# Layer 0 of a graph kernel: program order on VectorE, and twelve buffers of adj

## The chip, the cores and the metric

One core of one Trainium2 chip runs the whole program. The metric is device time in microseconds. Engines are named as in the profile: PE is TensorE's matmul row, PEld its weight loads, DVE VectorE, ACT ScalarE, POOL GpSimd, SP the engine that only issues transfers. DMA issues stand in the queues of SP, ACT and POOL beside their other work.

## The reference

Two graph layers over N = 4096 nodes with F = 512 features, one dense matrix `adj` with some 0.8% of its entries set (and the diagonal):

```python
# layer 0
h = relu(layernorm(x))
d = where(adj.sum(1) > 0, adj.sum(1) ** -0.5, 0)
x = x + relu((d[:, None] * adj * d[None, :]) @ h @ W0 + b0)
# layer 1
h = relu(layernorm(x))
g = h @ W1                                   # only g @ a[:F] and g @ a[F:] are used
e = leaky_relu((g @ a[:F]) + (g @ a[F:]).T, 0.2)
p = softmax(where(adj > 0, e, -1e12), axis=1)
q = -softmax(where(adj > 0, -e, -1e12), axis=1)
x = x + elu(concat([p @ h, q @ h], 1) @ wtrans)
```

## The kernel before

**Layer 0 is dense.** The 4096 output rows are 32 blocks of 128. The first phase (group 0, blocks 28 to 31) runs 32 rows of 128 nodes: for each it normalizes x on ACT and DVE, turns it on PE, multiplies it by W0 (`project`), and adds its product with the transposed adj into four PSUM banks (`multiply`). Beside that it streams the whole of `adj` in chunks of 128 x 1024 (`load_adj`, four a row, issued by SP into the pool `ain`): ACT sums a chunk (`junk`, line 747) for the degrees, DVE writes a 0/1 mark (line 748), and PE counts marks (`tally_up`) into a tally that says which nodes a half block of layer 1 needs. A chunk's buffer is free when its sum and its mark are done. The pool has 9 buffers.

Groups 1 to 8 (`GROUPS`: 4, 2, 4, 4, 4, 4, 4 and 2 blocks) compute the other 28 blocks by a Strassen scheme: for each of 16 steps jp, `load_at` brings the transposed adj (SP), `sum_at` makes four sums of its quarters on DVE (pool `sums`, three buffers; a two-block group makes them every second step), and `multiply_blocks` runs seven products for each pair of blocks on PE. A four-block group holds seven of the eight PSUM banks. When a group ends, the next one's first steps finish it: `join_blocks` puts its products together on DVE and `affine` scales them (group 0 needs `affine` alone, through `evict`), and at steps 0 to 3 `finish0` makes one block's x1 and its normalized row h: DVE and ACT take turns, ACT writes h (line 711, two buffers), two dots of h follow on DVE (line 895), h is written to one table by POOL's queue and to seven others by ACT's (line 465), and last DVE copies the second dot into t_all (line 905). A buffer of h is free when its eight writes have landed. The rows of the last two groups go to one table only. At step 12 `spread_s` turns s_all on PE (line 910) and sends it to memory.

Within a step the program traces the sums of step jp+1, at jp = 0 the joins, then the products of step jp, then `finish0`, then `step(jp)`.

**Lists.** `step` also takes items from two lists of work. `listing` holds, for each of two sides, eight beginnings (`block_codes` twice, `join_codes`, `count_nodes` four times, `make_places`), 73 rounds of `list_round`, and an end (`rows_and_joins`) for each of seven classes. A round finds the next eight entries of a class in each partition (lines 410 and 412) in a window of the 512 columns given by `place`. `joining` holds the transfers that POOL issues to put the lists into memory (`join`, line 432, each waiting for the one before) and `deal`, which brings them back and turns them into indices for layer 1.

**Layer 1 is sparse.** For each half block POOL gathers the listed rows of a table (line 473), DVE and ACT make the weights, and PE multiplies (line 516 and line 1397). The gathers of the first pair stand in group 8. A verdict, computed on the chip, says whether the lists were complete; if not, a dense layer 1 runs instead.

**Order.** The order of each engine's instructions is fixed when the program is compiled: a scheduler plays the program through with estimated times and takes what is ready, earlier traced work first. `keep_in_program_order(i)` ties i behind the one instruction that was traced just before it on its engine; it adds no wait of its own. Without it an instruction is placed where the scheduler finds its inputs ready.

**Weights.** `load_weights` loads a and W1 (transposed) by ACT's queue, at row 24 of the first phase; `weight_rows` multiplies them at row 30 (line 692) and spreads the result over all partitions as wa_bc (`wa`), which the dots of `finish0` read.

Of the kernel before, what the change touches and what calls it, by code (L numbers as in the profile page):

```python
# [19 lines left out]
P = 128  # L20
# [247 lines left out]
def gcn_gat_kernel(  # L268
# [118 lines left out]
    def place(c, n, side):  # L387


        p = SHARES[c]  # L390
        return (n + side * 8 * (n * (1 - p)) ** 0.5) / p

    def window(n):
        c, r = steps[n]
# [3 lines left out]
    def list_round(g, n):  # L398


        c, r = steps[n]
        if r == 0:
            keys[g] = make_pool.tile([P, EN], F32, tag="key", name=f"key{g}_{c}")
            lst[g] = make_pool.tile([P, max(CAPS)], F32, tag="lst", name=f"lst{g}_{c}")
            nc.vector.scalar_tensor_tensor(
                keys[g], codes[g], float(CODES[c]), rank, ALU.is_equal, ALU.mult
            )
        lo, hi = window(n)
        key, top = keys[g][:, lo:hi], lst[g][:, 8 * r : 8 * r + 8]
        nc.vector.max(top, key)  # L410
        if r + 1 < CAPS[c] // 8:
            nc.vector.match_replace(key, top, key, 0.0)

    def count_listed(g, c, lst):
        one = make_pool.tile([P, EN], F32, tag="flag16", name=f"listed{g}_{c}")[:, : CAPS[c]]
# [4 lines left out]

    def table_rows(g, c, lst):

        li = make_pool.tile([P, max(CAPS)], F32, tag="li", name=f"li{g}_{c}", bufs=2)
        li = li[:, : CAPS[c]]
        nc.vector.tensor_scalar(li, lst[:, : CAPS[c]], -1.0, base, ALU.mult, ALU.add)
        return li
# [11 lines left out]

    def deal(g):

        rows = make_pool.tile([P, EN], F32, tag="flag16", name=f"deal{g}")[:, : NH * STR // P]
        i = nc.gpsimd.dma_start(
            out=rows.rearrange("r (c p) -> r c p", p=P),
            in_=lst_dram[g].rearrange("(c r p) o -> r c (p o)", r=P, p=P),
        )
        turned = bank(f"deal_ps{g}")
        for c in range(NH * STR // P // P):
            part = slice(c * P, (c + 1) * P)
            nc.tensor.transpose(turned[:, part], rows[:, part], ident)
        nc.vector.tensor_copy(idx[g].rearrange("p b k -> p (b k)"), turned[:, : NH * STR // P])  # L450
        return i
# [108 lines left out]
    with sbuf(name="y0", bufs=1) as y_pool, sbuf(name="wa", bufs=1) as wa_pool, sbuf(name="bits", bufs=4) as bits_pool, sbuf(name="small0", bufs=4) as small, ExitStack() as rest, ExitStack() as lists:  # L560
# [109 lines left out]
            one(off[g], o, start, None, ALU.add)  # L670

        def load_bias(ln_pool):
            b_row = ln_pool.tile([1, F], F32, tag="b_row", name="b_row", bufs=1)
            nc.scalar.dma_start(out=b_row, in_=b0)
            nc.gpsimd.partition_broadcast(b_bc, b_row)

        def load_weights(ln_pool):

            a_sb = small.tile([P, 2 * FC], F32, tag="a_sb", name="a_sb", bufs=1)
            tc.keep_in_program_order(nc.scalar.dma_start(out=a_sb, in_=a_cols))  # L680
            w1t = []
            for c in range(FC):
                w1t.append(ln_pool.tile([P, F], F32, tag="w1t", name=f"w1t{c}", bufs=FC))
                tc.keep_in_program_order(
                    nc.scalar.dma_start(out=w1t[c], in_=w1_t[c * P : (c + 1) * P, :])
                )
            return a_sb, w1t

        def weight_rows(ln_pool, a_sb, w1t):
            wp = bank("wa_ps")  # L690
            for c in range(FC):
                nc.tensor.matmul(
                    wp[0:2, :], a_sb[:, c::FC], w1t[c], start=c == 0, stop=c == FC - 1
                )
            row = ln_pool.tile([2, F], F32, tag="wa_row", name="wa_row", bufs=1)
# [135 lines left out]

        def affine(y, acc, j):

            nc.vector.scalar_tensor_tensor(y, acc, d_all[:, j : j + 1], b_bc, ALU.mult, ALU.add)  # L834
            return y

        def new_y(work, j):
# [8 lines left out]
        def join_blocks(i0, n, acc, work, new_w):  # L846

            ys = {}
            for x in range(n // 2):
                p16, p23, p45, p7 = acc[x]  # L850
                j0, j1 = i0 + x, i0 + n // 2 + x
                ys[j0], ys[j1] = y, v = [new_y(work, j) for j in (j0, j1)]
                w = new_w(f"w{j0}")[:, :H]
                nc.vector.tensor_copy(y[:, :H], p16[:, :H])
                nc.vector.tensor_tensor(w, p16[:, H:], y[:, :H], ALU.add)  # L855
                nc.vector.tensor_tensor(y[:, H:], p45[:, H:], w, ALU.add)

                def first(p23=p23, y=y):
                    nc.vector.tensor_tensor(y, p23, y, ALU.add)  # L859

                def second(p7=p7, w=w, p45=p45, v=v):
                    two = "p (a f) -> p a f"
                    nc.vector.tensor_tensor(w, p7, w, ALU.add)
                    nc.vector.tensor_tensor(
                        v.rearrange(two, a=2),
                        p45.rearrange(two, a=2),
                        w.unsqueeze(1).to_broadcast([P, 2, H]),
                        ALU.add,
                    )
# [12 lines left out]
            return ys  # L882
# [70 lines left out]
        def sum_at(pool, at, n, name):  # L953

            a = blocks_of(at, n)
            q, w = a.shape[1], a.shape[4]
            t = pool.tile([P, 4, q, w], F32, tag="sums", name=name)
            op = nc.vector.tensor_tensor
            op(t[:, 0], a[:, :, 0, 1], a[:, :, 1, 1], ALU.add)
            op(t[:, 1], t[:, 0], a[:, :, 0, 0], ALU.subtract)  # L960
            op(t[:, 2], a[:, :, 0, 0], a[:, :, 0, 1], ALU.subtract)
            op(t[:, 3], a[:, :, 1, 0], t[:, 1], ALU.subtract)  # L962
            return t
# [34 lines left out]
                    seventh(x)  # L998

        i0, n = GROUPS[0]  # L1000
        with sbuf(name="w0", bufs=1) as w0_pool, sbuf(name="ain", bufs=9) as ain, sbuf(name="xs", bufs=5) as x_pool, sbuf(name="at6", bufs=5) as at_pool, sbuf(name="bits6", bufs=3) as bits6, sbuf(name="ln", bufs=3) as ln_pool, sbuf(name="marks", bufs=6) as mark_pool:
            dummy = ain.tile([P, RC], F32, tag="ain", name="dummy")
            dummy = dummy[:, : NH * STR // P]
            nc.gpsimd.memset(dummy, float(EN))
# [43 lines left out]
            for j in range(NJ):  # L1048
                tally_up(j)
                if j + 4 < NJ:  # L1050
                    load_x(x_pool, nc.gpsimd, j + 4)
                if j + 1 < NJ:
                    load_adj(ain, j + 1)
                    ats[j + 1] = load_at(at_pool, i0, n, j + 1, 1)
                    if j:
                        yps[j + 1] = project(w0_sb, j + 1)
                    sum_adj(j + 1, j < 3)
                if j == 3:
                    load_bias(ln_pool)
                if j == NJ - 8:  # L1060
                    vectors = load_weights(ln_pool)
                if j == NJ - 2:
                    weight_rows(ln_pool, *vectors)
                turn = partial(turn_x, ln_pool, j + 3, j < 2) if j < NJ - 3 else None
                multiply(acc, j, ats[j], turn)
                if j + 1 < NJ:
                    scale(yps.pop(j + 1), j + 1)
                pack(bits6, i0, j, ats.pop(j), j < 2)
        pending = (GROUPS[0], partial(evict, i0, acc))
        listing, joining = [], []  # L1070
        verdict = None
# [101 lines left out]
        with sbuf(name="work0", bufs=2) as work, sbuf(name="sums", bufs=3) as sum_pool, sbuf(name="at", bufs=6) as at_pool:  # L1173
# [29 lines left out]
        with sbuf(name="work2", bufs=2) as work, sbuf(name="sums2", bufs=2) as sum_pool, sbuf(name="at2", bufs=4) as at_pool, sbuf(name="scratch", bufs=1) as scratch, sbuf(name="pair", bufs=1) as pair:  # L1203
# [21 lines left out]
            def s_of0(r):  # L1225
                return s_pair[:, r % 2 * RB : (r % 2 + 1) * RB]

            def weights0(r):
# [274 lines left out]
```

## Time and profile before

| | us |
|---|---|
| median of 14 runs | 2152.63 (2143.09 to 2159.93) |
| the profiled execution | 2156.47 |
| its span | 2154.7 |
| first phase, to the first product of group 1 | 0 to 315.9 |
| groups 1 to 8 | 315.9 to 1056.9 |
| first half blocks of layer 1, from there | 1056.9 to 1170 |
| the rest of layer 1 | 1170 to 2154.7 |

PE is busy 1956.8 us (91%), DVE 1281.8 (59%), POOL 937.6 (44%), ACT 633.1 (29%). The page's digits by slices of 54 us:

```profile
PE   7998999889999999799865989989899999989988
PEld 3433348778788888688521333333333333333333
DVE  6554568979854388934443645655564546555561
...
PEclk9999999999999999999986999999999999999999
DMA  9887868386384747383758788888778888777760
```

Each digit is a tenth of busy share. Slices 0 to 5 are the first phase, slices 6 to 19 the groups, the rest layer 1. DVE is fullest in slices 6 to 10 and 15 to 16.

The rounds of the lists, and where they ran:

```profile
L410 DVE MAX8 lst<-key x146: 326/632/695, 371.4 to 897.3; 128x8 f32<-128x440 f32 x20, 128x8 f32<-128x480 f32 x14, 128x8 f32<-128x496 f32 x12, 128x8 f32<-128x488 f32 x12
...
busy tenths in 40 slices 0000000212100012200000000000000000000000
```

The three times are shortest, median and longest in ns. They fill slices 7 to 10 and 14 to 16 and are absent between: the scheduler has not spread them as the program lists them.

### The profile page before, as it was taken

How to read it: one execution, taken by the hardware profiler on the slowest of the kernel's cores; microseconds unless marked ns; L12 is line 12 of the kernel's file. 1: busy time of each engine (PE TensorE's matmuls, PEld its weight loads, DVE VectorE, ACT ScalarE, POOL GpSimd, SP SyncE). 2: the span in 40 equal slices, each digit the busy share in tenths (PEclk: the TensorE clock that was granted, in tenths of full speed). 3: DMA queues.
4: the chain of work that ended last, by engine and by line, in shares of the span. 5: the costliest groups of instructions: out<-in, count | busy, mean ns of one | idle time of the engine just before them, and what ended most of it. 6: DMA issues, size and time to landing. Idle time of an engine off the chain costs nothing.

```text
span 2154.7 us, 23721 instructions
## 1 busy us (share of the span) xinstructions
PE 1956.8 (91%) x7832; PEld 1079.9 (50%) x7832; DVE 1281.8 (59%) x2907; ACT 633.1 (29%) x1181; POOL 937.6 (44%) x1047
## 2 busy tenths in 40 slices
PE   7998999889999999799865989989899999989988
PEld 3433348778788888688521333333333333333333
DVE  6554568979854388934443645655564546555561
ACT  5765642112122212120221322322222223322221
POOL 3001001233321132331556667667666667766740
PEclk9999999999999999999986999999999999999999
DMA  9887868386384747383758788888778888777760
GB/s 364 308 302 263 301 207 311 92 265 216 100 312 139 269 160 254 98 282 97 228 172 290 244 279 254 268 272 254 259 249 268 252 276 254 238 248 247 238 196 21
DMA packets 181115, 503.53 MB, mean 234 GB/s; under 512 B 27091, under 2 KB 35699, under 8 KB 180982
## 3 DMA queue, kind: packets, MB, share of 16 engines
q0 software_dynamic: 73184, 275.36, 40.2%
q1 hardware_dynamic: 77808, 171.80, 23.6%
q10 hardware_dynamic: 29990, 54.75, 7.2%
q8 instruction: 64, 1.05, 0.2%
q14 instruction: 69, 0.57, 0.1%
HBM read 409.89 MB, written 103.02 MB: 238 GB/s over the span
## 4 chain that ended last, share of the span: by engine, by line
PE 43%; issue 5%; POOL 2%; DVE 1%; DMA 1%; ACT 0%; another core or an unknown queue 0%; DVEq 0%; POOLq 0%
PE u L516 31%; PE o L1397 10%; POOL g L473 2%; PE tp L550 2%; DMA g<-table,idx 0%; PE cs L540 0%; DMA table<-h 0%; DVE prod L895 0%; DVE stb L455 0%; DVE y L834 0%; DVE y L887 0%; DVE p L509 0%; POOL table L821 0%; ACT L499 0%; DVE y L859 0%
## 5 line engine op out<-in xcount | busy, mean ns | idle before, releaser
L473 POOL DMA_INDIRECT g<-table,idx x704 | 706.4, 1003 | 326.6 <-issue 207.6
L516 PE MATMUL u<-g,p 128*64 128x512 f32 x2816 | 701.7, 622 | 94.2 <-issue 77.6
L516 PEld LDWEIGHTS u<-g,p 128*64 128x64 f32 x2816 | 214.9, 142 | 525.1 <-issue 503.1
L972 PE MATMUL p<-t,sums 128*128 128x256 f32 x896 | 268.4, 384 | 12.3 <-DVE sums L960 7.8
L972 PE MATMUL p<-y,at 128*128 128x256 f32 x896 | 272.3, 386 | 2.3 <-DVE w L855 1.2
L972 PE MATMUL p<-y,sums 128*128 128x256 f32 x896 | 270.6, 384 | 0.4 <-DVE sums L962 0.4
L1397 PE MATMUL o<-wt_sb,ut 128*128 128x512 f32 x512 | 225.4, 593 | 0.5 <-ACT ut L555 0.5
L432 POOL DMA_INDIRECT ld<-li,off x112 | 101.7, 908 | 255.1 <-DMA ld<-li,off 196.6
L812 ACT ACTIVATE m<-at 128x1024 uint8<-128x1024 f32 x110 | 115.0, 1053 | 331.3 <-DMA at<-in_adj_t 273.9
L1367 DVE TENSOR_REDUCE total<-p 128x128 f32<-128x1792 f32 x62 | 201.9, 3257 | 2.1
L972 PEld LDWEIGHTS p<-t,sums 128*128 128x128 f32 x896 | 171.6, 193 | 40.3 <-DVE sums L960 11.1
L972 PEld LDWEIGHTS p<-y,at 128*128 128x128 f32 x896 | 171.3, 193 | 30.1 <-issue 2.7
L972 PEld LDWEIGHTS p<-y,sums 128*128 128x128 f32 x896 | 172.8, 193 | 25.1 <-DVE sums L962 0.8
L509 DVE SCALAR_TENSOR_TENSOR p<-g,p 128x384 f32<-128x384 uint8 (+1 forms) x256 | 145.5, 618 | 26.3 <-issue 13.8
L747 ACT ACTIVATE junk<-ar 128x1024 bf16<-128x1024 f32 x128 | 134.7, 1052 | 73.9 <-DMA ar<-in_adj 72.6
L821 POOL DMA_DIRECT2D table<-m x71 | 56.5, 796 | 225.4 <-ACT m L812 138.7
L1397 PEld LDWEIGHTS o<-wt_sb,ut 128*128 128x128 f32 x512 | 94.8, 190 | 108.5 <-issue 107.0
L1383 ACT ACTIVATE us<-u,rl 128x512 f32<-128x512 f32 x62 | 42.6, 688 | 360.0 <-PE u L516 145.7
L1405 DVE TENSOR_SCALAR eo<-o 128x512 f32<-128x512 f32 x32 | 22.1, 691 | 211.3 <-remote 80.0
L972 PE MATMUL p<-t,at 128*128 128x256 f32 x448 | 135.7, 385 | 9.8 <-DVE w L855 8.7
L487 DVE TENSOR_TENSOR z<-g,s 128x512 f32<-128x512 f32 (+1 forms) x124 | 77.8, 628 | 112.2 <-DMA g<-table,idx 97.3
L499 ACT ACTIVATE p<-z 128x512 f32<-128x512 f32 (+2 forms) x252 | 123.4, 548 | 70.4 <-issue 38.4
(198 smaller groups left out, 1937.5 us busy)
## 6 DMA issues: line engine op xcount, KB each, us to landing
ar<-in_adj SPq DMA_DIRECT2D x128, 512.0 KB
at<-in_adj_t SPq DMA_DIRECT2D x112, 512.0 KB
table<-h ACTq DMA_DIRECT2D x182, 258.0 KB
table<-m POOLq DMA_DIRECT2D x55, 256.0 KB
g<-table,idx POOLq DMA_INDIRECT x704
at<-in_adj_t SPq DMA_DIRECT2D x32, 256.0 KB
xr<-in_x SPq DMA_DIRECT2D x32, 256.0 KB
x1d<-y POOLq DMA_DIRECT2D x32, 256.0 KB
```

The source lines that it names most:

```text
L432: return nc.gpsimd.indirect_dma_start(out=lst_dram[g][:, :], out_offset=bass.IndirectOffsetOnAxis(ap=off[g][:, e, c : c + 1], axis=0), in_ ...
L473: i = nc.gpsimd.indirect_dma_start(out=gt[:, k, :], out_offset=None, in_=table[2 * n // RPT], in_offset=bass.IndirectOffsetOnAxis(ap=idx[n ...
L487: return nc.vector.tensor_tensor(z, t.to_broadcast([P, n, RB]), s.unsqueeze(1).to_broadcast([P, n, RB]), ALU.add)
L499: i = nc.scalar.activation(p[:, :, :, g], z, AF.Exp, scale=(1.0, -1.0)[g])
L509: nc.vector.scalar_tensor_tensor(e, m, 0.0, e, ALU.is_gt, ALU.mult)
L516: i = nc.tensor.matmul(u[h * RB : (h + 1) * RB], p[:, k, h].rearrange("p g i -> p (g i)"), row(k), start=k == HALVES[r % 2][h][0], stop=en ...
L747: nc.scalar.activation(junk, ar, AF.Identity, accum_out=part[:, c : c + 1]),
L812: nc.scalar.activation(m, at, AF.Sign)
L821: nc.gpsimd.dma_start(out=rows_of(t, e)[:, c:, ROW_W + (a - t * TT) * P // 4 : ROW_W + (b - t * TT) * P // 4], in_=masks[i0][:, c:, (a - i ...
L972: i = nc.tensor.matmul(out, left[:, x * P : (x + 1) * P], right, start=jp == 0 and first, stop=jp == NP - 1 and (final or not first),)
L1367: nc.vector.tensor_reduce(total, q, AX.X, ALU.add)
L1397: nc.tensor.matmul(po, ut[:, g, c, :], wt_sb[:, g * FC + c, :], start=g == 0 and c == 0, stop=g == 1 and c == FC - 1,)
```

## The change

1. `list_round`'s two instructions, `affine`, every instruction of `join_blocks` and the four of `sum_at` are tied to program order, and so are the scores of the second half block in `weights0` at the end of layer 0.
2. The pool `ain` has 12 buffers. To make room, the four W1 tiles take `ain` buffers and two short rows share one buffer. `load_weights` moves from row 24 to row 30, `weight_rows` behind the loop.
3. The lower edge of a round's window is 6 instead of 8 deviations from the mean; the upper stays at 8.
4. One list item a step is taken in group 2 too, where none was, and two joins a step always, where it was one or two. `li` has three buffers, and `deal` has a tile of its own.

```diff
-        return (n + side * 8 * (n * (1 - p)) ** 0.5) / p
+        return (n + side * (7 + side) * (n * (1 - p)) ** 0.5) / p
...
-        nc.vector.max(top, key)
+        tc.keep_in_program_order(nc.vector.max(top, key))
         if r + 1 < CAPS[c] // 8:
-            nc.vector.match_replace(key, top, key, 0.0)
+            tc.keep_in_program_order(nc.vector.match_replace(key, top, key, 0.0))
...
-        li = make_pool.tile([P, max(CAPS)], F32, tag="li", name=f"li{g}_{c}", bufs=2)
+        li = make_pool.tile([P, max(CAPS)], F32, tag="li", name=f"li{g}_{c}", bufs=3)
...
-        rows = make_pool.tile([P, EN], F32, tag="flag16", name=f"deal{g}")[:, : NH * STR // P]
+        rows = make_pool.tile([P, NH * STR // P], F32, tag="deal", name=f"deal{g}")
...
-        def load_weights(ln_pool):
+        def load_weights(ain):
...
-                w1t.append(ln_pool.tile([P, F], F32, tag="w1t", name=f"w1t{c}", bufs=FC))
+                w1t.append(ain.tile([P, RC], F32, tag="ain", name=f"w1t{c}")[:, :F])
...
-            nc.vector.scalar_tensor_tensor(y, acc, d_all[:, j : j + 1], b_bc, ALU.mult, ALU.add)
+            tc.keep_in_program_order(
+                nc.vector.scalar_tensor_tensor(y, acc, d_all[:, j : j + 1], b_bc, ALU.mult, ALU.add)
+            )
...
+            def op(*args):
+                tc.keep_in_program_order(nc.vector.tensor_tensor(*args))
+
...
-                nc.vector.tensor_copy(y[:, :H], p16[:, :H])
-                nc.vector.tensor_tensor(w, p16[:, H:], y[:, :H], ALU.add)
-                nc.vector.tensor_tensor(y[:, H:], p45[:, H:], w, ALU.add)
+                tc.keep_in_program_order(nc.vector.tensor_copy(y[:, :H], p16[:, :H]))
+                op(w, p16[:, H:], y[:, :H], ALU.add)
+                op(y[:, H:], p45[:, H:], w, ALU.add)
...
             t = pool.tile([P, 4, q, w], F32, tag="sums", name=name)
-            op = nc.vector.tensor_tensor
+            def op(*args):
+                tc.keep_in_program_order(nc.vector.tensor_tensor(*args))
+
...
-        with sbuf(name="w0", bufs=1) as w0_pool, sbuf(name="ain", bufs=9) as ain, sbuf(name="xs", bufs=5) as x_pool, sbuf(name="at6", bufs=5) as at_pool, sbuf(name="bits6", bufs=3) as bits6, sbuf(name="ln", bufs=3) as ln_pool, sbuf(name="marks", bufs=6) as mark_pool:
+        with sbuf(name="w0", bufs=1) as w0_pool, sbuf(name="ain", bufs=12) as ain, sbuf(name="xs", bufs=5) as x_pool, sbuf(name="at6", bufs=5) as at_pool, sbuf(name="bits6", bufs=3) as bits6, sbuf(name="ln", bufs=3) as ln_pool, sbuf(name="marks", bufs=6) as mark_pool:
...
-                if j == NJ - 8:
-                    vectors = load_weights(ln_pool)
                 if j == NJ - 2:
-                    weight_rows(ln_pool, *vectors)
+                    vectors = load_weights(ain)
...
                 pack(bits6, i0, j, ats.pop(j), j < 2)
+            weight_rows(ln_pool, *vectors)
...
-                    n = 0 if b == 2 or not 0 < jp < 14 else 1 if b == 1 else 2 + jp % 2
-                    for todo, n in ((listing, n), (joining, 1 + jp % 2)):
+                    n = 0 if not 0 < jp < 14 else 1 if b < 3 else 2 + jp % 2
+                    for todo, n in ((listing, n), (joining, 2)):
...
-                    scores(s_of0(r), z[:, k : k + n], gt[:, :, ROW_T : ROW_T + 1].bitcast(F32))
+                    i = scores(s_of0(r), z[:, k : k + n], gt[:, :, ROW_T : ROW_T + 1].bitcast(F32))
+                    if r == blocks[1]:
+                        tc.keep_in_program_order(i)
```

More of the change, by code (lines that the diff above doesn't have):

```diff
@@ L672, in load_bias @@
         def load_bias(ln_pool):
-            b_row = ln_pool.tile([1, F], F32, tag="b_row", name="b_row", bufs=1)
+            b_row = ln_pool.tile([1, F], F32, tag="row", name="b_row", bufs=1)
             nc.scalar.dma_start(out=b_row, in_=b0)
             nc.gpsimd.partition_broadcast(b_bc, b_row)
-        def load_weights(ln_pool):
+        def load_weights(ain):
             a_sb = small.tile([P, 2 * FC], F32, tag="a_sb", name="a_sb", bufs=1)
@@ L694, in weight_rows @@
                 )
-            row = ln_pool.tile([2, F], F32, tag="wa_row", name="wa_row", bufs=1)
+            row = ln_pool.tile([2, F], F32, tag="row", name="wa_row", bufs=1)
             nc.scalar.copy(row, wp[0:2, :])
@@ L853, in join_blocks @@
                 w = new_w(f"w{j0}")[:, :H]
-                nc.vector.tensor_copy(y[:, :H], p16[:, :H])
-                nc.vector.tensor_tensor(w, p16[:, H:], y[:, :H], ALU.add)
-                nc.vector.tensor_tensor(y[:, H:], p45[:, H:], w, ALU.add)
+                tc.keep_in_program_order(nc.vector.tensor_copy(y[:, :H], p16[:, :H]))
+                op(w, p16[:, H:], y[:, :H], ALU.add)
+                op(y[:, H:], p45[:, H:], w, ALU.add)
                 def first(p23=p23, y=y):
-                    nc.vector.tensor_tensor(y, p23, y, ALU.add)
+                    op(y, p23, y, ALU.add)
                 def second(p7=p7, w=w, p45=p45, v=v):
                     two = "p (a f) -> p a f"
-                    nc.vector.tensor_tensor(w, p7, w, ALU.add)
-                    nc.vector.tensor_tensor(
+                    op(w, p7, w, ALU.add)
+                    op(
                         v.rearrange(two, a=2),
```

## The prediction

> **What bounds the kernel now.** I read the page first (PE busy 91%, its last digits full), then the waits of TensorE, then a table by stage, cut where the traced blocks of layer 0 begin. Its columns are stretch, length, busy time with instruction counts of PE, weight loads, DVE, ACT, POOL, then granted clock, DMA share and GB/s.
>
> ```profile
> 43.90:93.10 49.20, 48.97 (x172) 21.05 (x172) 28.71 (x96) 35.77 (x77) 5.16 (x7) 1.00 0.91 336
> 93.10:312.00 218.90, 202.75 (x649) 83.09 (x652) 117.12 (x335) 132.30 (x262) 15.72 (x23) 0.99 0.79 267
> ...
> 315.90:424.60 108.70, 100.96 (x469) 87.17 (x468) 100.31 (x298) 24.81 (x29) 20.76 (x31) 0.95 0.64 215
> 424.60:483.70 59.10, 51.75 (x227) 44.41 (x226) 47.96 (x142) 10.84 (x17) 20.49 (x28) 0.91 0.78 256
> 483.70:585.70 102.00, 98.56 (x452) 84.70 (x451) 93.99 (x245) 19.78 (x22) 39.41 (x49) 1.00 0.49 160
> 585.70:687.50 101.80, 99.38 (x451) 85.89 (x450) 49.20 (x139) 20.69 (x25) 15.76 (x26) 0.98 0.63 215
> 687.50:785.80 98.30, 98.30 (x473) 85.87 (x472) 59.70 (x188) 20.68 (x25) 22.84 (x34) 1.00 0.64 215
> 785.80:891.30 105.50, 100.09 (x451) 85.67 (x450) 92.68 (x259) 20.47 (x25) 31.76 (x45) 0.98 0.59 200
> 891.30:1002.40 111.10, 101.06 (x455) 86.51 (x453) 47.59 (x140) 16.12 (x21) 29.27 (x41) 0.97 0.51 172
> ```
>
> The first two rows are the first phase, the others groups 1 to 7. Group 5, at 98.3 us, is a four-block group in which PE never waits; a two-block group would take half, 49.2. Against this, groups 1 to 7 lose 10.4, 9.9, 3.7, 3.5, 0, 7.2 and 12.8 us, together 47.5. They lose where DVE is nearly always busy (100.3 of 108.7 us in group 1) or stood full of list rounds just before. The longest waits of PE are:
>
> ```profile
> PE p L972 <- DVE w L855: 9.9, 4, 6.7
> PE s_ps L910 <- DVE prod L895: 7.4, 1, 7.4
> PE s_ps L910 <- DVE o L669: 7.3, 1, 7.3
> ```
>
> So VectorE's order costs layer 0 up to 47 us. From 1170 us the digits show PE full; the later layer moves as a block, by when group 8 ends.
>
> In the first phase a row of 128 adj rows has 28 matmul records (counts, yp and acc 8 each, tx 4). The fast stretch does 172/28 = 6.1 rows at 8.0 us; the long one, less the 8 records of wa_ps, 641/28 = 22.9 rows at 9.56, with a DMA share of 0.79. The queue of SP tells why:
>
> ```profile
> SPq L735 <- DVE mark L748: 169.9, 72, 7.7
> ...
> 208.86 2.13 SPq L735 DMA_DIRECT2D ar<-in_adj  x4
> ```
>
> The columns of a wait are total, times, longest; those of the timeline start and length. Four loads leave together here, and the next at 218.95, 10.1 us on, when a batch of marks frees their buffers; ACT then waits for them (3.11 us at 213.80), its row sum waits, d_all waits, and the next marks stand behind d_all on DVE. It is a loop through the buffers.
>
> **Twelve buffers.** Chunk 4x+3 of adj now waits for the mark of 12 chunks earlier, not 9, so for one batch of marks earlier: the loop opens. Bounds per row: nothing, if DMA is the limit, to 9.56 - 8.0 = 1.56 us, the rate of the fast stretch (34 us over 22 to 23 rows). From 100 to 125 us the share is 0.88 at 293 GB/s, only a tenth above the long stretch's 267; I take 0.83 us a row, between the ends: 23 x 0.83 = **-19 us**.
>
> **The weights, moved.** load_weights goes from row 24 to row 30: five ACT issues, past the ACT work of six rows; 0, for the weights are wanted only after the last row. weight_rows goes behind the loop: its eight matmul records (304.62 to 308.2, 3.6 us of PE) run once as before, its ACT copy (0.58) and three ACT issues go past one row: 0. But wa_bc lands later: now the copy is at 308.25 and its two broadcasts are issued at 311.38. Moved behind the last matmul (316), the first dot of group 1, some 11 us in, just covers it; without that cover it costs 0 to 4. SP's loads for group 1 today wait 15.6 us for wa_ps, whose weights lie where those loads land. If the first load still does, PE waits for landing (308.24 to 312.25) and two sums, 4.8 us. Between 0 and 8.8 in all: **+2**.
>
> **Lists.** A round is (88.0 + 78.0 + 11.7)/146 = 1.22 us of DVE, by the busy times of lines 410 and 412. The narrower lower edge takes the columns that one side's rounds scan, by the formula, from 59,592 to 53,616; at 1.06 ns a column (0.35 us for 184 columns at 818.10, 0.68 for 496 at 850.73) that is 12.7 us of DVE for both sides, 1.13 us a round; it is hidden behind PE except where a round stands in a sum below. Each side has 73 rounds, 7 ends and 8 beginnings, 176 items in all. They go at 1 a step in groups 1 and 2, then 2 or 3, and end in group 7. The lists' third li buffer removes a DVE wait of 4.08 us (at 879.49, inside group 6's loss). Deal's own tile: nothing of DVE waits for it by the trace; 0.
>
> **The pins.** The losses above should shrink, since rounds no longer crowd. But a pinned instruction follows the DVE instruction traced just before it. The sums of step k stand behind finish0 of step k-2 (its last DVE instruction copies t_all) and that step's list rounds. The copy waits for a dot, the dot for ACT's h, and h for the buffer that eight table writes must leave. Group 5 shows the times:
>
> ```profile
> 697.24 0.15 DVE L905 COPY t_all<-h 128x1 f32<-128x1 f32 x1
> ...
> 708.24 0.15 DVE L905 COPY t_all<-h 128x1 f32<-128x1 f32 x1
> ...
> 713.45 0.14 DVE L905 COPY t_all<-h 128x1 f32<-128x1 f32 x1
> ...
> 722.39 0.81 ACT L711 ACTIVATE h<-y,rrb 128x512 f32<-128x512 f32 x1 [10.94 <-DMA table<-h]
> ...
> 724.64 0.15 DVE L905 COPY t_all<-h 128x1 f32<-128x1 f32 x1
> ```
>
> That is 9.7, 20.7, 26.0 and 37.1 us after the group's first product. A step lasts 98.3/16 = 6.1 us; PE wants two sums (0.8 us) of step 5 at 30.9. Behind the fourth copy and three rounds (3.4) they come at 37.1 + 3.4 + 0.8 = 41.3: 10.4 us late, where today those sums ran at 714.5, 27 us in. Bounds for the fourth copy: if ACT issues the second tile's seven writes right after the first's (6.1 us each set, landing 7.3 us after, by 703.2 and the wait that ends at 710.5), it falls to about 32.8, 6.1 us late; at 42.5 (groups 4 and 6) 15.8. I take 35, between group 5's row and the better order: 8.3 late.
>
> Each such wait also lowers the clock: the 1.96 us wait at 588.65 is followed by a granted 0.86 over 586 to 598, so 3.4 us at half, 1.7 lost. Two waits a group: 3.4. A head then costs 11.7.
>
> The Trainium skill, in "TensorE: Matmul & The Clock Gate" under "HAM oscillation — how this bites in real kernels", has it that only idle gaps above about 3.4 us bring the slow clock back. The 1.96 us row differs from it (a 2.05 us wait at 946.68, with a clock of 1.00 after it, agrees). By the rule waits of 2 to 3 us cost no clock, and the total below would be an estimated 14 us less.
>
> Groups 4 to 7: 4 x 11.7 = 46.8 against 23.5 lost now: **+23** (+8 to +60). Group 2, of two blocks, has steps of 3.07 us: its fourth set of sums, wanted at 18.8, stands behind the fourth copy and two rounds: 35 + 2.3 + 0.8 = 38.1, 19.3 late, 5 of clock, 9.9 lost now: **+14** (+11 to +24). Group 3 has two tiles, so only the second copy bites (18 to 20.7, plus 4.2, against 18.7, and 1.7): 5 to 8 against 3.7: **+2** (-2 to +5). Group 1 has no rounds yet in its head; its four affines now stand behind the second sums, whose load ended DVE's wait at 318.42, 2.5 in, and hold four PSUM banks until then, up to 3; its fourth copy comes 35 to 41 in, 4.9 to 10.9 late, with clock 8 to 14, against 10.4 lost now: **0** (-6 to +10). Group 8 sets the end through its tables, not PE: its joins end 10 us in, against 4.6 in group 5, and the pinned joins go first; and DVE's 5.92 us wait for a gather at 1070.55 now stands behind the late tiles' work instead of ahead of it: **-8** (-11 to 0).
>
> Sum: -19 + 2 + 23 + 14 + 2 + 0 - 8 = **+14**, on the profiled execution's own 2156.47 us (span 2154.7 and 1.8 around it): 2170.5. The runs' median, 2152.63, is 3.8 lower: **2167 us**.
>
> **Rivals.**
> - ACT's better order, 26%. Pinned dots come in order, so the second tile's writes precede the third's h; against it, the trace has them after in group 5. It decides from a fourth copy at 33 us or sooner. Low ends for the groups (+11), 25 us from the first phase, -9 at the tail: -23, **2130 us**.
> - The pins are free, 12%: what is late in the trace is mostly crowding. The 47.5 us go but for 1 us at each boundary (-40), -17 and -8: **2088 us**. Against it: group 5 had no rounds in its head and its fourth copy was 37.1 late.
> - Twelve buffers do nothing, 22%: DMA is full at the rate of 100 to 125 us. Without the 19: +33, **2186 us**. For it: 0.88 is near the 0.91 of the fast stretch.
> - POOL falls behind, 8%. Two joins a step at 0.91 us and a 2.2 us wait each (196.6/89) fill 6.2 of 6.1 us; the memset of h stands behind them and the table writes behind it. One step, 6 us, in five heads: +30, **2197 us**.
> - All cancels, 7%.
>
> The forecast itself has 25%, from 2157 to 2186. Slower: 25 + 22 + 8 = 55%; faster 26 + 12 = 38%; the same, within 0.2% (about 4 us, what this measurement tells from nothing), 7%. The range is 2100 to 2230: the cases' bounds, less their outer tenths.
>
> **What would show it.** Right: rows of the first phase near 8.7 us and SP's wait for marks well under 170; PE waits for sums in the heads of groups 2 and 4 to 7, each ended by sums that start right after a t_all copy or a round; no wait for s_ps of 7 us; rounds up to about 900 us. Wrong: heads without waits (then the fourth copy is early, or sums run ahead of it); row times still 9.5. If a list missed an entry at the narrower edge, the dense layer would run and the time would be far outside.

## The result, and the profile after

| | before | after |
|---|---|---|
| median of the runs | 2152.4 us (47 runs) | 2181.26 us (10 runs, 2172.78 to 2201.58) |
| the profiled execution | 2156.47 | 2180.4 |
| its span | 2154.7 | 2178.6 |

The ratio of after to before is 1.0139, with a 95% interval from 1.0118 to 1.0159: the changed kernel is 29 us slower. The forecast was 2167 us, 14 slower. Between the two profiled executions lie 23.9 us; the other 5 are their places beside their medians (before 4.1 above, after 0.9 below). The stages below are of these two executions.

The table by stage of the changed kernel has the columns of the one before. It is cut where the first product of each group starts; the first row is the long stretch of the first phase, the last one group 8, and group 3 is left out.

```profile
93.10:309.30 216.20, 201.41 (x658) 83.80 (x657) 116.53 (x329) 133.58 (x266) 16.60 (x25) 0.98 0.77 264
309.30:415.80 106.50, 102.40 (x468) 87.27 (x469) 73.83 (x235) 25.41 (x30) 13.72 (x23) 0.97 0.67 223
415.80:485.80 70.00, 53.42 (x228) 44.69 (x228) 46.16 (x129) 12.26 (x17) 16.59 (x26) 0.88 0.67 227
...
584.20:693.70 109.50, 103.56 (x452) 89.30 (x451) 90.61 (x243) 20.39 (x25) 34.11 (x46) 0.94 0.57 192
693.70:803.40 109.70, 101.24 (x472) 87.16 (x471) 78.00 (x229) 20.36 (x25) 30.93 (x44) 0.97 0.59 198
803.40:908.80 105.40, 99.55 (x451) 86.06 (x450) 77.16 (x222) 20.50 (x25) 26.06 (x36) 0.98 0.60 202
908.80:1026.00 117.20, 103.43 (x454) 88.98 (x453) 61.28 (x175) 16.27 (x21) 32.54 (x47) 0.94 0.49 161
1026.00:1099.70 73.70, 53.85 (x229) 44.51 (x229) 38.85 (x102) 15.43 (x21) 33.47 (x40) 0.91 0.68 215
```

DVE is less full where it was fullest (group 1: 73.8 us of 106.5, before 100.3 of 108.7), and its rounds lie further apart: the ties did spread them. Yet groups 2, 4, 5 and 7 are 11, 8, 11 and 6 us longer. Stage by stage, with the forecast's terms:

| stage | before | after | change | forecast |
|---|---|---|---|---|
| first phase, to the first product of group 1 | 315.9 | 309.3 | -6.6 | -17 |
| group 1 | 108.7 | 106.5 | -2.2 | 0 |
| group 2 | 59.1 | 70.0 | +10.9 | +14 |
| group 3 | 102.0 | 98.4 | -3.6 | +2 |
| groups 4 to 7 | 416.7 | 441.8 | +25.1 | +23 |
| group 8 and all behind it | 1152.3 | 1152.6 | +0.3 | -8 |
| sum | 2154.7 | 2178.6 | +23.9 | +14 |

The waits of TensorE after (total, times, longest):

```profile
PE p L980 <- DVE sums L965: 54.2, 17, 11.2
PE deal_ps L449 <- DMA deal<-ld: 14.5, 2, 7.5
...
PE p L980 <- DMA at<-in_adj_t: 9.4, 2, 6.6
```

The waits for `s_ps` and for `w`, which were the longest in the groups before (some 7 us each), are down to 1.6 us or none. In their place stand 17 waits for sums (before there were 10, 12.7 us together), and two kinds that were not there at all: for the deal, and for the first load of group 1. The queue of SP after:

```profile
SPq L735 <- DVE mark L748: 151.0, 67, 8.4
```

The last round starts at 967 us, later than the 900 foreseen, and SP still waits 151 us for marks. A row of the first phase took 9.0 us (209.6 us to 302.7, 650 records at 28 a row; before 9.56).

### The profile page after: what moved, and what is told of

It reads as the page before. It is cut to its first block, busy times and chain, and to the rows that moved or that the text cites. A ratio compares the mean times of both kernels' runs of the same rounds, so it can differ in the third digit from the quotient of the medians.

```text
span 2178.6 us, 23743 instructions
## 1 busy us (share of the span) xinstructions
PE 1956.8 (90%) x7832; PEld 1090.4 (50%) x7832; DVE 1283.5 (59%) x2907; ACT 632.6 (29%) x1181; POOL 935.8 (43%) x1047
## 3 DMA queue, kind: packets, MB, share of 16 engines
q0 software_dynamic: 73184, 275.36, 39.7%
## 4 chain that ended last, share of the span: by engine, by line
PE 40%; issue 6%; POOL 4%; DMA 2%; DVE 1%; ACT 0%; another core or an unknown queue 0%; POOLq 0%; DVEq 0%; SPq 0%; ACTq 0%
PE u L516 28%; PE o L1406 9%; POOL g L473 3%; PE tp L550 2%; PE p L980 1%; DMA g<-table,idx 1%; DMA ld<-li,off 1%; PE cs L540 0%; DVE p L509 0%; DMA x1d<-y 0%; DVE prod L901 0%; DMA table<-m 0%; DMA at<-in_adj_t 0%; DMA deal<-ld 0%
## 5 line engine op out<-in xcount | busy, mean ns | idle before, releaser
L516 PE MATMUL u<-g,p 128*64 128x512 f32 x2816 | 692.4, 617 | 84.2 <-issue 72.0
L980 PE MATMUL p<-y,sums 128*128 128x256 f32 x896 | 276.9, 392 | 35.0 <-DVE sums L965 35.0
L980 PE MATMUL p<-t,sums 128*128 128x256 f32 x896 | 274.0, 392 | 21.7 <-DVE sums L965 19.3
L509 DVE SCALAR_TENSOR_TENSOR p<-g,p 128x384 f32<-128x384 uint8 (+1 forms) x256 | 145.6, 619 | 23.6 <-issue 14.5
L965 DVE TENSOR_TENSOR sums<-at 128x256 f32<-128x256 f32 x224 | 93.4, 418 | 110.2 <-PE p L980 98.4
```

The costliest lines, as they stand in the source:

```text
L509: nc.vector.scalar_tensor_tensor(e, m, 0.0, e, ALU.is_gt, ALU.mult)
L516: i = nc.tensor.matmul(u[h * RB : (h + 1) * RB], p[:, k, h].rearrange("p g i -> p (g i)"), row(k), start=k == HALVES[r % 2][h][0], stop=en ...
L965: tc.keep_in_program_order(nc.vector.tensor_tensor(*args))
L980: i = nc.tensor.matmul(out, left[:, x * P : (x + 1) * P], right, start=jp == 0 and first, stop=jp == NP - 1 and (final or not first),)
```

## Three places in the trace after

**The head of a group (4).** First DVE, lines of its timeline; a bracket is the idle time before a line and what ended it.

```profile
597.33 0.69 DVE L893 SCALAR_TENSOR_TENSOR y<-y,xr 128x512 f32<-128x512 f32 x1 [3.36 <-DMA xr<-in_x]
...
598.55 0.15 DVE L911 COPY t_all<-h 128x1 f32<-128x1 f32 x1
598.62 0.41 DVE L965 TENSOR_TENSOR sums<-at 128x256 f32<-128x256 f32 x1
...
610.37 0.25 DVE L708 SCALAR_TENSOR_TENSOR rrb<-mvb,rrb 128x1 f32<-128x1 f32 x2 [3.32 <-ACT rrb L707]
...
613.53 0.15 DVE L911 COPY t_all<-h 128x1 f32<-128x1 f32 x1
...
620.25 0.41 DVE L965 TENSOR_TENSOR sums<-at 128x256 f32<-128x256 f32 x1
```

TensorE wants the sums of step 2 at 596.9. They start at 598.62, right behind the first t_all copy, and that copy is late because DVE stood 3.36 us at an instruction of the *third* tile, which waits for its x. That one is not tied, so the scheduler put it where it expected the load to have landed; the tied sums cannot pass it. The sums of step 4 stand behind the third tile's copy and its rounds. There DVE waits for ACT, whose queue shows why:

```profile
594.39 15.70 ACTq L465 DMA_DIRECT2D table<-h  x14
610.14 0.29 ACT L707 ACTIVATE rrb<-rrb 128x1 f32<-128x1 f32 x2 [14.79 <-DMA table<-h]
```

The fourteen table writes of the first two tiles go out in one row, 1.1 us each, and the square root of the next tiles stands behind them.

**The end of the first phase.** SP issues the first x and adj_t loads of group 1 as soon as the products of wa_ps, which stand behind the last row, have read the W1 tiles; TensorE has nothing until one lands:

```profile
299.11 3.60 PE L692 MATMUL wa_ps<-w1t,a_sb 128*2 128x512 f32 x8
...
302.78 0.80 SPq L830 DMA_DIRECT2D xr<-in_x  x2
...
303.68 0.90 SPq L925 DMA_DIRECT2D at<-in_adj_t  x2
...
309.31 1.22 PE L980 MATMUL p<-y,at 128*128 128x256 f32 x2 [6.61 <-DMA at<-in_adj_t]
```

The rows themselves ended at 302.7 and not at 315.9, so 13 us were won and 6.6 given back at once, and more through the clock: the stretch from 305.8 to 316.0 ran at a granted 0.50, 6.7 us of it behind the wait, so 3.4 us of work were lost there.

**Group 8.** Its sums of step 12 are traced behind the weights of the first half block of layer 1:

```profile
1077.83 0.69 DVE L487 TENSOR_TENSOR z<-g,s_pair 128x512 f32<-128x512 f32 x1 [5.80 <-DMA table<-m]
...
1086.03 0.41 DVE L965 TENSOR_TENSOR sums<-at 128x256 f32<-128x256 f32 x1
```

Tied, they wait until that half block's gathered rows are there and its weights are made. (The profile puts the 5.80 us down to `table<-m`, a write in the same POOL queue; the instruction itself reads the gathered `g`.) TensorE stood from 1078.9 for 7.6 us.

## The experiments

Every ratio is to the kernel before, on the same chip, with its 95% interval. The first four ran where that kernel took 2160 us; the others on chips where it took 2028, so they are compared with the changed kernel by the ratio (its own is 1.0139). The expectations in us go with a kernel before of 2152. The changed kernel itself did not run on those chips; that its ratio is the same there is taken, not shown.

**e1: the sums untied.**

```diff
-            def op(*args):
-                tc.keep_in_program_order(nc.vector.tensor_tensor(*args))
+            op = nc.vector.tensor_tensor
             op(t[:, 0], a[:, :, 0, 1], a[:, :, 1, 1], ALU.add)
```

> The changed kernel with the four instructions of sum_at no longer tied to program order; rounds, joins and affine stay tied. Theory A (the tied sums are what costs: TensorE waits 54.2 us for sums in 17 places, and some 54 us at half clock follow those waits, which is 27 us of work lost): the waits in the heads of groups 2 and 4 to 8 go, groups 4 to 7 come near 100 us each and group 8 near 55, time 2110 to 2130. Rival B (the sums are late because DVE is crowded by rounds, wherever they are put): waits for sums stay above 35 us, time 2165 to 2185.

2154.8 us, ratio 0.9969 [0.9946, 0.9992]: the four ties of `sum_at` cost 1.7%, some 36 us, with the longer waits for the deal, which untying brought, already taken off. No wait for sums is left in the heads, and groups 2, 4 and 6 run without a wait. The time is above theory A's because the waits for the deal grew:

```profile
656.50:784.70 128.20, 101.30 (x473) 86.65 (x472) 79.25 (x234) 20.58 (x25) 39.85 (x52) 0.91 0.52 171
```

```profile
PE deal_ps L449 <- DMA deal<-ld: 44.7, 2, 25.6
```

Group 5 (the row of the table) waits 25.6 us for its deal, group 7 another 19.1. The deal hangs on POOL's chain of joins; when TensorE comes sooner, it only waits longer.

**e2: the first phase alone, on the kernel before** (twelve buffers, `load_weights` at row 30 into the adj buffers, `weight_rows` behind the loop, one tag for the two rows).

> The kernel before with the changes of the first phase alone: twelve buffers, load_weights at row 30, weight_rows behind the loop, the rows of b and wa in one tag. Theory A (rows gain about 13 us, and the switch to group 1 gives some 7 of it and more back, since its first loads stand behind wa_ps): group 1 begins near 309, time 2140 to 2148. Rival B (what group 1 gains in its start it loses in its head or later): 2150 to 2156. Rival C (twelve buffers are worth the forecast 19 us): 2132 to 2138.

2164.83 us, ratio 1.0014 [0.9989, 1.0039]. The rows ended at 296.9 us and not at 315.9: just the 19 us of the forecast. Then came a wait of 7.29 us, group 1 began at 304.2 and was 4.6 us longer, and nothing of the gain was left at the end. Rival B's figure held, though its reason is not the whole of it (e9).

```profile
93.10:296.90 203.80, 197.83 (x660) 82.73 (x657) 114.93 (x325) 133.48 (x264) 15.55 (x24) 1.00 0.79 273
...
304.20:417.50 113.30, 102.44 (x469) 87.79 (x470) 101.29 (x304) 24.27 (x29) 19.68 (x30) 0.94 0.62 209
```

```profile
304.20 1.22 PE L972 MATMUL p<-y,at 128*128 128x256 f32 x2 [7.29 <-DMA at<-in_adj_t]
```

**e3: none of the ties** on rounds, joins, affine and sums; the rest as changed.

> The changed kernel with none of the ties on rounds, joins, affine and sums (the tie on the scores of the second half block stays); the buffers, the pace of the lists, the deal's tile and li's third buffer stay as changed. Theory A (the ties are the whole loss): 2140 to 2155, with the s_ps waits of 7 us and more back. Rival B (the pace of rounds and joins, two joins a step, costs by itself, through deals that TensorE waits for): above 2165.

2163.9 us, ratio 1.0011 [0.9987, 1.0035], which is 2155 against 2152, the upper end of theory A; and no wait for the deal stands in its profile, so rival B's mechanism is not there. The waits for `s_ps` (9.5 us with the tail's, and 8.9 in group 1) and for `w` (16.8) were back. The ties together cost 1.3%. Those on rounds, joins and affine alone (e1) give 0.4% against none, some 7 us with an uncertainty of 4 on the same chip, with 44.7 us of waits for deals in it.

**e4: the deal's transposes later.**

```diff
-                    joining.append(partial(deal, g))
+                    joining.append(lambda: dealt.update({g: deal(g)}))
+                    joining.extend([lambda: None] * 5)
+                    joining.append(partial(turn_deal, g, dealt))
```

> The changed kernel with deal cut in two: its transfer is issued as before, its transposes on TensorE and the copy into idx are traced six items of the joining list (three steps) later. Theory A (the two waits of 7.0 and 7.5 us for the deal in groups 5 and 7, with 6.8 us at half clock behind each, lie on the path): time 2158 to 2165, no wait of PE for deal. Rival B (the time that TensorE gains is lost again at the next sums, which stand behind the list rounds anyway): 2174 to 2182.

2177.59 us, ratio 1.0063 [1.004, 1.0086], some 16 us under the changed kernel. Group 7 lost its wait (117.2 to 109.9 us); in group 5 6.3 us of wait remained:

```profile
721.71 0.82 POOL L442 DMA_DIRECT2D deal<-ld  x1 [5.63 <-DMA ld<-li,off]
...
737.46 0.34 DVE L672 TENSOR_SCALAR o<-o_ps,begin 16x8 f32<-16x8 f32 x2
...
737.90 0.87 PE L453 MATMUL deal_ps<-ident,deal 128*128 128x128 f32 x3 [6.27 <-issue]
```

The transfer had left 16 us before; in the changed kernel TensorE began 3 to 6 us after it. The profile names no releaser, but TensorE begins just as DVE ends its last read of `o_ps`, and `o_ps` and `deal_ps` take their bank from the same PSUM pool, of which a four-block group leaves one. DVE had stood 13.56 us for h before that. Theory A holds for group 7 and, nearly, in size: the ratio makes 2166 against 2152, 1 us over its range.

**e5: the sums untied in group 8 alone.**

> The changed kernel with the ties of sum_at taken off in group 8 alone, where they put the sums of step 12 behind the weights of the first half block and those of step 3 behind a finished tile (TensorE waits of 7.6 and 6.8 us, half clock after both). Theory A (group 8's end is set by the tables, the gathers and the late tiles, so what TensorE loses there is covered by the slow stretch that follows): group 8 shortens from 73.7 to about 55 to 60 us, the gathers of layer 1 move by less than 4 us, time 0 to 5 us under the changed kernel, ratio to before 1.011 to 1.014. Rival B (TensorE's 24 us in group 8 count): 12 us less or more, ratio 1.008 or under.

Ratio 1.0100 [1.0076, 1.0123]. Group 8 fell from 73.7 to 54.4 us, 19 less, and the time by 0.4%, some 8 us with an uncertainty of about 6: between the theories. e6 and e7 below ran on the same chip with these sums tied, and bear it out: from the first product of group 8 to the last product of gathered rows, their profiled executions took 1007.9 (1027.9 to 2035.8) and 1007.5 us (1073.3 to 2080.8), that of e5 997.5 (1027.3 to 2024.8), 10 less. So about half of what TensorE loses there is covered. In e5 TensorE then stands 5.5 us before its first product of layer 1, a wait that the changed kernel does not have:

```profile
PE u L516 <- DVE p L509: 5.5, 1, 5.5
```

**e6: three buffers of h.**

> The changed kernel with three buffers of h instead of two in groups 1 to 7. Theory A (the third and fourth t_all copies are late because h waits for the table writes of two tiles before): the third copy falls from 29 to about 20 us, the sums of step 4 come in time, the waits of 1.2 to 3.8 us behind them in groups 4, 6 and 7 and part of the 11.2 us of group 2 go, 20 to 30 us less than the changed kernel, ratio 1.000 to 1.005. Rival B (fourteen table writes in a row in ACT's queue hold the square root of the third tile, 14.8 us in group 4, whatever the buffers are): copies at 28 to 30 us as before, ratio 1.011 to 1.016.

Ratio 1.0128 [1.0102, 1.0155], the same. ACT's queue in group 4:

```profile
612.63 0.30 ACT L707 ACTIVATE rrb<-rrb 128x1 f32<-128x1 f32 x2 [15.23 <-DMA table<-h]
```

Rival B: the third copy came at 30.0 us into the group (29.3 before the edit). It is ACT's queue that holds the third tile, not the buffer. The buffer was not worth nothing, though: the fourth copy came 2 us earlier in groups 4, 6 and 7, and all waits for sums fell from 54.2 to 44.7 us, while those for the deals rose from 14.5 to 27.7 and took it back.

**e7: no list items in steps 1 to 3.**

> The changed kernel with no list items in steps 1 to 3 of a group (the lists then end later). Theory A (the sums are late behind the t_all copies; the rounds add 1.1 us each): the waits for sums in groups 2 and 4 to 7 keep half or more of their 40 us, ratio 1.005 to 1.013. Rival B (it is the rounds that stand in front of the sums): waits for sums under 15 us, ratio under 1.003, unless the later lists cost it back in group 8.

Ratio 1.0376 [1.0347, 1.0405]. The waits, total, times, longest:

```profile
PE deal_ps L449 <- DMA deal<-ld: 62.4, 1, 62.4
PE p L980 <- DVE sums L965: 57.2, 21, 8.2
```

With no round in front of them the sums are waited for as long as before (57.2 against 54.2): theory A on the cause, the t_all copies. Its time was missed, because the lists then end 60 us after TensorE reaches their deal in group 7.

**e9: e2 with weight_rows earlier.**

```diff
+                if j == NJ - 2:
+                    weight_rows(ln_pool, *vectors)
                 turn = partial(turn_x, ln_pool, j + 3, j < 2) if j < NJ - 3 else None
                 multiply(acc, j, ats[j], turn)
...
-            weight_rows(ln_pool, *vectors)
```

> The kernel before with the changes of the first phase alone, as in e2, but weight_rows called before the products of row 30 and not behind the loop. Theory A (the switch to group 1 costs 12 us: 7.3 of wait, because the first loads of group 1 stand behind wa_ps, and half of 6.8 to 10.2 us at half clock): wa_ps ends some 7.7 us earlier against the end of the phase, the wait falls under 2 us, group 1 begins near 297, ratio to before 0.993 to 0.997. Rival B (what the first phase gains is lost later in layer 0 or at the gathers): group 1 begins near 297, but the ratio is 0.999 to 1.003.

Ratio 0.9955 [0.994, 0.9971]: theory A.

```profile
287.95 3.60 PE L692 MATMUL wa_ps<-w1t,a_sb 128*2 128x512 f32 x8
...
299.19 0.59 PE L972 MATMUL p<-y,at 128*128 128x256 f32 x2
```

wa_ps stands 11 us before the end of the rows, SP's loads left at 291.6, and TensorE goes from row to group without a gap. The same twelve buffers, worth nothing in e2, are worth 0.45%, about 9 us; between the two ratios lie 0.59%, some 12 us.

**e8, e10, e11, e12: towards a better kernel.** e8 is the changed kernel with the sums untied, `weight_rows` as in e9, the first deal's transposes twelve joining items later, and the second deal in layer 1:

```diff
             for k, r in enumerate(order):
                 product(r)
+                if k == 6:
+                    x0 = work.tile([P, F], F32, tag="x1", name="deal0")[:, : NH * STR // P]
+                    deal(0, x0, nc.sync)
+                if k == 9:
+                    turn_deal(0, x0)
```

> The changed kernel with sum_at untied, weight_rows called before the products of row 30 (so that the loads of group 1 no longer stand behind the last row), the transposes of the first deal traced twelve joining items later, and the second deal moved into layer 1, where its indices are first wanted. Theory A (the ties on rounds and joins are a gain that the tied sums, the deals and the switch to group 1 hide): no wait of TensorE for deal, none of 7 us at the start of group 1, group 8 begins near 925 to 940, time 65 to 75 us under the untied-sums kernel, ratio 0.962 to 0.970. Rival B (the tables and gathers set the start of layer 1, whatever layer 0 does): ratio 0.98 to 0.99.

1981.39 us against 2027.83, ratio 0.9770 [0.9747, 0.9793], between the two theories. What each of its edits brings is not separated: 0.45% is the first phase by e9, and the other 1.85% the ties on rounds, joins and affine together with the other changes of the lists, the deals out of the way. Group 8 began at 955.7, not at 925 to 940: group 5 alone took 118.6 us, with a wait of 16.3 us. Two tries at it, e10 with one or two joins a step, and e11 with h's zeros written by ACT:

> e8 with one or two joins a step as before, not two. Theory A (in e8 POOL falls behind: the zeroing of h for the third tile of group 5 stands behind the joins of side 1, DVE waits 26.1 us for h and TensorE 16.3 for the sums behind it): that wait goes, group 5 falls from 118.6 to under 103 us, 15 to 25 us under e8, ratio 0.963 to 0.970. Rival B (slower joins end later and hold the gathers of group 8): group 5 falls, but gathers begin more than 15 us later against the start of group 8, ratio 0.975 or more.

> e10 with the three columns of h zeroed by ACT (a copy with a scale of 0) and not by a memset on POOL. Theory A (the memset behind the joins is what ties h to POOL): first to fourth t_all copies of groups 4 to 7 come 2 to 10 us earlier, but TensorE hardly waits there any more, so 0 to 4 us under e10. Rival B (ACT's own queue of table writes delays the zeroing): the same as e10 within 2 us, or slower.

Ratios 0.9753 [0.9728, 0.9778] and 0.9763 [0.9736, 0.9790]: no difference to e8 that can be told, and group 5 still 117.4 and 113.3 us. Neither theory of e10 held: the pace is not it. POOL and DVE in e10's group 5:

```profile
693.72 0.81 POOL L440 DMA_DIRECT2D deal<-ld  x1 [1.37 <-DMA ld<-li,off]
...
695.32 1.65 POOL L893 DMA_DIRECT2D x1d<-y  x3
696.95 0.55 POOL L464 DMA_DIRECT2D table<-h  x1
```

```profile
701.76 0.69 DVE L900 SCALAR_TENSOR_TENSOR prod<-h,wa 128x512 f32<-128x512 f32 x1 [24.97 <-ACT h L710]
```

The scheduler had placed the joins and the deal ahead of the x1 and table writes of two tiles whose h was written at 662 and 669 us; h's buffers wait for those writes, and DVE for h. e12 ties each join behind them:

```diff
-        return nc.gpsimd.indirect_dma_start(
+        i = nc.gpsimd.indirect_dma_start(
...
+        tc.keep_in_program_order(i)
+        return i
```

> e10 with each join tied to program order on POOL too, behind the x1 and table writes of finish0 in the same step. Theory A (in group 5 it is POOL's order that makes h late: thirteen joins and the deal stand before the x1 and table writes of the first two tiles, whose buffers of h the third tile wants): the 15.5 us wait of TensorE in group 5 falls under 4 us, group 5 under 104 us, 12 to 20 us under e10, ratio 0.966 to 0.970. Rival B (joins that stand behind writes start later, so the lists end later and hold the gathers of group 8): group 5 falls, but the time stays at 0.973 to 0.980.

1974.43 us against 2028.95, ratio 0.9734 [0.9718, 0.9750], the best measured (its interval overlaps those of e8 and e10).

```profile
649.60:751.00 101.40, 99.44 (x473) 85.44 (x472) 79.59 (x236) 20.57 (x25) 26.32 (x37) 1.00 0.65 216
```

Group 5 is 101.4 us, theory A's mechanism; group 8 begins 13.7 us earlier than in e10, but joins now run until 971 us, into group 8, whose gathers begin only 5.8 us earlier (988.2 against 994.0). That part, and the ratio, are rival B's.

## Why the prediction was right or wrong

The direction was right, and so was the main mechanism: tied sums stand behind work that waits, and TensorE behind them. The size was half. Between the profiled executions the sum gave 14 and 23.9 were measured. Two terms failed, each by 8 us: the weights, moved (10.0 for +2), and group 8 with the tail (+0.3 for -8). The twelve buffers gained 6 less than forecast in this execution, groups 4 to 7 lost 2 more, and groups 1 to 3 came out 14 us better (apart from the 3.4 us of clock of the weights' term, which lie in group 1), so that these cancel in part.

**The weights, moved (+2; bounds 0 to 8.8).** The step named the danger, that SP's first load might still stand behind wa_ps, and then took nearly nothing for it. It did stand there: 6.6 us of wait and 3.4 for the clock make 10.0, above the upper bound, which had left the clock out. e2 and e9 show that this term decides whether the first phase gains anything: 1.0014 with it, 0.9955 without.

**Twelve buffers (-19).** 19.0 us in e2, to the figure, and 13.2 in the changed kernel. The thirteen profiled executions with twelve buffers ended their rows between 296.9 (e2) and 305.9 us, at 301.5 on average, so 14 us is the fairer figure, and that e2 hits 19 is luck. The row of 8.7 us came in e2 (203.8 us over 652/28 rows, 8.75), not in the changed kernel (9.0). SP's wait for marks fell only to 151 us, not "well under 170": the loop opened by one batch but did not vanish.

**Group 8 and the tail (-8; measured +0.3).** The step looked at what the ties move forward (the joins) and not at what stands traced in front of the tied sums of step 12, a half block's weights with a gather. e5 puts the cost of the ties in group 8 at some 8 us, and the traces of one chip at 10. The slack that the step counted on covers the rest of the 19. The +0.3 itself is loose: from the first to the last product of gathered rows, the six executions on the slower chips (before, after, e1 to e4) took 1053 to 1080 us, so one pair tells the tail to no better than some 10 us.

**Groups 4 to 7 (+23; measured +25) and 2 (+14; +10.9): right sums of other parts, so by luck.** Each wait for sums is ended by sums that start behind a t_all copy, as said, and e1 shows that these ties cost most of all. The fourth copy came at 35.3, 39.7, 32.6 and 34.1 us, against the 35 taken. But the cause written down was the h buffer; e6 shows that for the third tile it is the row of fourteen writes in ACT's queue. The trace before had it too: the prediction's line of h at 722.39 comes as soon as ACT has issued the twelve writes in front of it.

```profile
711.49 10.78 ACTq L465 DMA_DIRECT2D table<-h  x12
```

The 8.3 us at step 5 did not come, since an unpriced wait at step 2 and its slow clock had already put TensorE back. Waits for sums and s_ps in groups 4 to 7 add up to 19.5 us, with 11 more for the clock: 30, against 46.8. **The deal, priced 0**, filled the gap. Before, POOL issued the two deals at 595.4 and 963.1 us, and TensorE turned them at 760.8 and 1001.5: 165 and 38 us of slack. After, the rounds, spread further, bring the lists later, and the deals leave at 715.1 and 1008.4; but the program, at two joins a step, meets the first one sooner, at step 3 of group 5. In group 7:

```profile
1011.46 0.87 PE L449 MATMUL deal_ps<-ident,deal 128*128 128x128 f32 x3 [7.53 <-DMA deal<-ld]
```

Two such waits, 14.5 us, and 4.4 for the clock make 19; e4, in which 6.3 us of wait were left, measured 16. The step asked whether DVE waits for the deal, and TensorE was the one that did.

**Groups 1 and 3 (0 and +2; measured -2.2 and -3.6).** Group 1 is inside its range. Group 3 is below its lower end of -2: its one wait for sums lasted 0.9 us, where 5 to 8 us of loss were forecast.

**The rivals.** "ACT's better order" had the copies nearly right and the time wrong. By its own sign, a fourth copy at 33 us or sooner, it came in group 6 alone (32.6); copies did not set the end. "The pins are free" is refuted by e1. "Twelve buffers do nothing" named 2186, nearest to the measured time, by a wrong reason: the rows did gain, the switch gave it back. "POOL falls behind" was put at 8%; in the changed kernel it shows in group 5 alone, and with the sums untied it is the largest wait left (e8 to e12).

What stays open: why e2 kept nothing at the end of the 5.5 us it still had at group 8 (it ran where the kernel before took 2160 us and not 2152, and no profile shows that kernel there), and what the ties on rounds and joins are worth without the other edits of e8.

## What to carry to other kernels

A tie to program order is as good as the slowest thing traced before it: rounds and joins, tied behind a tile's end, gained some 7 us (e1 against e3), while sums that TensorE waits for lost 36 behind work that waits for ACT, for x or for a gather. Tie filler work, and leave what the busiest engine waits for free. When a gain moves a phase's end forward, check what the next phase's first loads stand behind, and price every consumer of a chain whose producers are not made faster: here it was TensorE that waited for the deal.

## What the runs showed of the hardware

**The clock.** Windows of the changed kernel at six waits; the third number from the end is the granted clock.

```profile
305.80:316.00 10.20, 6.43 (x14) 4.71 (x15) 7.32 (x20) 2.93 (x3) 1.86 (x3) 0.50 0.97 322
338.20:345.00 6.80, 4.37 (x21) 3.85 (x21) 6.80 (x20) 1.88 (x3) 1.40 (x3) 1.00 1.05 373
438.90:452.50 13.60, 4.61 (x11) 3.40 (x12) 8.53 (x26) 2.87 (x5) 1.95 (x4) 0.50 0.89 318
816.10:823.00 6.90, 4.89 (x24) 4.32 (x24) 6.90 (x26) 0.00 (x0) 1.63 (x3) 1.00 1.04 371
923.60:927.00 3.40, 2.98 (x7) 2.44 (x8) 3.40 (x14) 0.00 (x0) 0.54 (x1) 0.50 1.05 373
1008.90:1015.70 6.80, 4.24 (x12) 3.55 (x13) 1.98 (x5) 0.00 (x0) 0.47 (x4) 0.50 0.08 29
```

They go with waits of 6.61, 2.43, 11.17, 2.01, 2.53 and 7.53 us, which ended at 309.3, 340.7, 447.9, 818.1, 924.0 and 1011.5. In the four rows with half clock it begins inside the wait and outlasts it by 3.0 to 6.7 us, so that it costs 1.5 to 3.4 us of work, where the forecast took 1.7 for each. The Trainium skill, in "TensorE: Matmul & The Clock Gate" under "HAM oscillation — how this bites in real kernels", asks for idle gaps of no more than some 3.4 us; here the wait of 2.53 us came with half clock, and those of 2.43 and 2.01 did not. With the 1.96 us of the prediction's row, which did, no single length divides them. The 14 us that the prediction takes off by that rule count both waits of a head as short, though one of them, 8.3 us by its own sum, is not.

**Chips differ.** The kernel before took 2152 and 2160 us in two of the measurements, and 2028 to 2029 (medians) on three other chips. The groups are alike (group 5, without a wait, 98.3 us on both); layer 1 is not. Its last 2100 products of gathered rows took 753.3 us at a granted 0.96 in the first, and 669.9 at 1.00 in e9, whose layer 1 is the same, on one of the three. Four hundredths of 753.3 are 30 us, so the clock explains at most that of the 83; the rest is not explained by these runs.
